# Four-layer sparse graph network on one core: the order of a block's two halves, and feed-forward rows in two buffers

## The chip, the cores and the metric

The kernel runs on one core of one Trainium2 chip. The metric is the device time of one execution in microseconds, given as the median of several runs. The core has a matrix engine (TensorE, in the profile PE, with its weight loads shown apart as PEld), three engines for vectors (VectorE, in the profile DVE; ScalarE, ACT; GpSimd, POOL), and queues that start transfers (SP's queue and GpSimd's). Each engine works through its own list of instructions, and semaphores tie the lists together.

## What is computed

The input is 16 graphs' states on 1024 shared nodes with 128 features, and one 1024 by 1024 adjacency matrix of zeros and ones with about 8 neighbours a node. Four layers follow one another. Layers L0, L2 and L3 are graph transformers with 8 heads of 16, layer L1 is a graph attention layer with one head:

```python
# L0, L2, L3
Q, K, V = h @ Wq, h @ Wk, h @ Wv                 # 8 heads of 16
attn = softmax(where(adj == 0, -inf, Q K^T / sqrt(16)))
x = layer_norm(h + (attn @ V) @ Wo + bo) * ln1_g + ln1_b
y = relu(x @ W1 + b1) @ W2 + b2                  # 128 -> 256 -> 128
x = layer_norm(x + y) * ln2_g + ln2_b
# L1
h = x @ W;  e = leaky_relu(h @ a_src + (h @ a_dst)^T, 0.2)
x = layer_norm(softmax(where(adj == 0, -inf, e)) @ h + x) * ln_gamma + ln_beta
```

## The kernel before

**Tiling.** The kernel works sparsely. A setup turns the adjacency matrix into lists of neighbours, with nodes sorted by degree. After that, a *unit* is one layer, one of two groups of eight graphs, and one of eight tiles of 128 nodes: 4 x 2 x 8 = 64 units in sequence. Within a unit each node's neighbours are handled in *parts* (about six or seven for an attention unit): `gathered` fetches the key and value rows of up to two neighbours a node from a table in DRAM by indirect DMAs (issued by GpSimd, L856), `products` multiplies them by the query on VectorE (L868), `exponentials` sums over each head on VectorE (L891) and takes the exponential on ScalarE (L895), `weighted` multiplies the value rows by it on VectorE (L919), and `summed` adds the rows of a node on TensorE with matrices of marks (L935). When a unit has no more parts, `divided` sums the exponentials on TensorE and divides on VectorE (L972, L975).

**What sets the order.** Everything is written out by hand under a manual schedule; the order of the program is the order of each engine's list. The main loop runs over the parts. Between a part's steps it calls `others()` three times in an attention unit and four times in a graph unit. `others()` opens the *tails* (the rest of the previous unit's layer) at a pace that spreads 15 steps (8 in the graph layer) over the unit, and one further generator (`fronts`: queries of the next unit; `loads`; or `slow`, the second group's entry). A tail is a Python generator, and each `yield` ends a step. `advance(gens)` takes every generator of a list one step further; one such call is an *opening* here.

**Halves and steps.** Each unit has two tails, for its two halves of four graphs: A is h = 0, B is h = 1. B begins with one empty step, so it stands one step behind A. The steps of `attention_tail` are, with the profile's lines:

- 0: transposes of the attention's result (TensorE, L596), copy oT (ScalarE, L598), bias on the layer's input (ScalarE, L640)
- 1: eight matmuls with Wo and the centring matrix into the PSUM tile yps (L644, L645)
- 2: four squares with sums (ScalarE, L580); 3: reciprocal root rstd (GpSimd, L586); 4: four scalings z (ScalarE, L589)
- 5: transposes of z (L596), copy x1 with gain and shift (ScalarE, L600)
- 6: two matmuls with W1 (L655) and two Relus (ScalarE, L659) into the feed-forward rows f1
- 7: eight matmuls with W2 (L664) and four with the centring matrix (L668) into yps
- 8, 9, 10: as 2, 3, 4, for the second norm
- 11: transposes of z, copy xT (L600)
- 12: the store of xT (SP, L530), two matmuls for keys and values and their copy (L538, L542); 13: two more; 14: the store into the next layer's table (SP, L547). In the last layer, 12 transposes back (L596, L598) and 13 writes the output (an indirect DMA of GpSimd, L625).

A matmul in float32 stands in the trace as two records. `graph_tail` has a shorter list: matmuls, squares, rstd, z, then the steps from 11 on with three copies in place of one (L558, L559).

In an opening, the kernel before takes A's step k and then B's step k - 1. So A7 is issued in front of B6, A6 in front of B5, and so on. All feed-forward rows share one buffer: B6's Relus write the rows that A7 has read.

**Other buffers that the change touches.** The pool `smalls` has three buffers for the scores sc, the graph layer's of and the pair both of sums and reciprocals; `exps` has two buffers of exponentials, of 16 x 64 numbers a partition, though a unit needs at most 12 x 64. The larger size is there because the setup's entry (`at_once`, eight blocks, both halves at the same step) borrows these buffers for the second half's keys and values.

Of the kernel before, what the change touches and what calls it, by code (L numbers as in the profile page):

```python
# [12 lines left out]
F32 = mybir.dt.float32  # L13
# [7 lines left out]
P = 128  # L21
D = 128
H = 8
HD = 16
FF = 256
F = FF // P
# [17 lines left out]
G = B // GR  # L44
HF = 2
GH = G // HF
# [4 lines left out]
J = P // 32  # L51
# [37 lines left out]
MOST = max(sum(map(len, _pieces)) for _pieces in PIECES)  # L89
# [33 lines left out]
def sparse_path(ctx: ExitStack, tc: tile.TileContext, a: dict, out: bass.AP, flag):  # L123
# [50 lines left out]
    reps = ctx.enter_context(tc.tile_pool(name="reps", bufs=2))  # L174
    ones_ = ctx.enter_context(tc.tile_pool(name="ones_", bufs=1))
    twos = ctx.enter_context(tc.tile_pool(name="twos", bufs=2))
    exps = ctx.enter_context(tc.tile_pool(name="exps", bufs=2))
    scratch = ctx.enter_context(ExitStack())
    s1 = scratch.enter_context(tc.tile_pool(name="s1", bufs=1))
# [425 lines left out]
    def finish(l, g, t, h, z, gain, shift):  # L605
# [22 lines left out]
            in_=o.rearrange("p g d -> p (g d)"), in_offset=None,  # L628
        )

    def attention_tail(l, g, t, h, o):
        layer = LAYERS[l][0]
        p = {n: w[layer, n] for n in ATTN if (layer, n) in w}
        xt = xs[l, g, t][:, h]
        for _ in range(h):
            yield
        oT = twos.tile([P, GH, P], F32, tag="oT", name="oT")
        turned(o, oT)

        nc.scalar.activation(xt, xt, AF.Identity, bias=p["bo"])  # L640
        yield
        ps = ybanks.tile([P, GH, D], F32, tag="yps", name="yps")
        for i in range(GH):
            nc.tensor.matmul(ps[:, i, :], oT[:, i, :], p["Wo"], start=True, stop=False)  # L644
            nc.tensor.matmul(ps[:, i, :], xt[:, i, :], centre, start=False, stop=True)  # L645
        yield
        z = yield from normed(ps)
        yield
        x1 = twos.tile([P, GH, P], F32, tag="oT", name="x1")
        turned(z, x1, p["ln1_g"], p["ln1_b"])  # L650
        yield
        f1 = ones_.tile([P, F, GH * P], F32, tag="f1", name="f1")
        for f in range(F):
            ps = bank([P, GH * P])
            nc.tensor.matmul(  # L655
                ps, p["W1"][:, f * P : (f + 1) * P], x1.rearrange("p g n -> p (g n)"),
                start=True, stop=True,
            )
            nc.scalar.activation(f1[:, f, :], ps, AF.Relu, bias=p["b1"][:, f : f + 1])  # L659
        yield  # L660
        ps = ybanks.tile([P, GH, D], F32, tag="yps", name="yps")
        for i in range(GH):
            for f in range(F):
                nc.tensor.matmul(  # L664
                    ps[:, i, :], f1[:, f, i * P : (i + 1) * P], p["W2"][:, f, :],
                    start=(f == 0), stop=False,
                )
            nc.tensor.matmul(ps[:, i, :], x1[:, i, :], centre, start=False, stop=True)  # L668
        yield
        z = yield from normed(ps)  # L670
        yield
        yield from finish(l, g, t, h, z, p["ln2_g"], p["ln2_b"])
# [55 lines left out]
    def at_once(g):  # L728

        spare = reps.tile([P, J, ROW], F32, tag="qr", name="spare")  # L730

        def fetch(t):
            if t < T:
                nc.sync.dma_start(
                    spare[:, t % J, :], a["x"][t * P : (t + 1) * P, columns(g, 0, HF)]
                )

        for t in range(3):
            fetch(t)
        yield  # L740
        for t in range(T):
            fetch(t + 3)
            rows = spare[:, t % J, :].rearrange("p (h g d) -> p h g d", h=HF, g=GH)
            both = []
            for h in range(HF):
                kv = None
                if h:
                    kv = exponents()[:, : 2 * GH * D].rearrange("p (c g d) -> p c g d", c=2, g=GH)
                both.append(natural(g, t, h, rows[:, h], kv))
            while both:  # L750
                advance(both)
                yield

    def exponents():
        return exps.tile([P, max(MOST, 2 * D // HD) * G * H], F32, tag="ex", name="ex")


    units = [(l, g, t) for l in range(len(LAYERS)) for g in range(GR) for t in range(T)]
# [40 lines left out]
    def queries(u):  # L799

        l, g, t = units[u]
        if not is_attention(u):
            ps = bank([P, J + 1, G])
            for j in range(J):
                nc.tensor.matmul(ps[:, j, :], rep_of(j, True), srcs[g, t], start=True, stop=True)
            for k, j in enumerate(SHARED[t]):
                at = slice(64 * k, 64 * k + 64)
                nc.tensor.matmul(
                    ps[at, MIX, :], rep_of(j, True)[:, at], srcs[g, t], start=True, stop=True
                )  # L810
            ofs[u] = smalls.tile([P, J + 1, G], F32, tag="of", name="of")
            nc.scalar.copy(ofs[u], ps)
            return
        qs[u] = reps.tile([P, J, ROW], F32, tag="qr", name="qr")
        for h in range(HF):
            q = ones_.tile([P, GH * D], F32, tag="q", name="q")
            ps = bank([P, GH, D])
            for i in range(GH):
                nc.tensor.matmul(
                    ps[:, i, :], xs[l, g, t][:, h, i, :], w[LAYERS[l][0], "Wq"],  # L820
                    start=True, stop=True,
                )
            nc.scalar.copy(q, ps.rearrange("p g d -> p (g d)"))
            yield
            pss = []
            for j in range(J):
                ps = bank([P, GH * D])
                nc.tensor.matmul(ps, rep_of(j), q[32 * j : 32 * j + 32], start=True, stop=True)  # L828
                pss.append(ps)
            for j in range(J):  # L830
                nc.scalar.copy(qs[u][:, j, h * GH * D : (h + 1) * GH * D], pss[j])  # L831
            yield
# [49 lines left out]
    def exponentials(i):  # L882
        u, pieces = parts[i]
        t = units[u][2]
        heads = H if is_attention(u) else 1
        sc = smalls.tile([P, es[i].shape[1], G * heads], F32, tag="sc", name="sc")
        if u not in exs:
            exs[u] = exponents()[:, : MOST * G * heads].rearrange("p (c a) -> p c a", a=G * heads)
        ex, n = exs_of(i)
        if is_attention(u):  # L890
            nc.vector.tensor_reduce(  # L891
                sc[:, :n, :], prs[i][0][:, :n, :].rearrange("p k (a d) -> p k a d", d=HD),
                mybir.AxisListType.X, ALU.add,
            )
            nc.scalar.activation(ex, sc[:, :n, :], AF.Exp, scale=1.0 / HD**0.5)  # L895
        else:
            k = 0
            for piece in pieces:
                m = k + len(piece)
                nc.vector.tensor_tensor(  # L900
                    sc[:, k:m, :], es[i][:, k:m, ROW:], of_piece(ofs[u], piece), ALU.add
                )
                k = m
            nc.vector.scalar_tensor_tensor(
                sc[:, :n, :], sc[:, :n, :], SLOPE, sc[:, :n, :], ALU.mult, ALU.max
            )
            nc.scalar.activation(ex, sc[:, :n, :], AF.Exp)
# [55 lines left out]
    def divided(u):  # L963

        l, g, t = units[u]
        heads, d = (H, HD) if is_attention(u) else (1, D)
        den = bank([P, G * heads])
        for n, c in enumerate(sum(PIECES[t], [])):
            marked(t, c, den, exs[u][:, n, :])
        both = smalls.tile([P, 2, G * heads], F32, tag="both", name="both")  # L970
        yield
        nc.vector.reciprocal(both[:, 1, :], den)  # L972
        for h in range(HF):
            o = twos.tile([P, GH, D], F32, tag="o", name="o")
            nc.vector.tensor_tensor(  # L975
                o.rearrange("p g (a d) -> p (g a) d", d=d),
                accums[u][:, h, :].rearrange("p (a d) -> p a d", d=d),
                both[:, 1, h * GH * heads : (h + 1) * GH * heads]
                .rearrange("p (a o) -> p a o", o=1)
                .to_broadcast([P, GH * heads, d]),  # L980
                ALU.mult,
            )
            tails.append((attention_tail if heads > 1 else graph_tail)(l, g, t, h, o))
        nc.scalar.copy(both[:, 0, :], den)
        n = G * heads
        nc.gpsimd.tensor_tensor(seen[:, :, :n], seen[:, :, :n], both, ALU.add)
# [4 lines left out]
    slow = []  # L991

    def advance(gens):
        for gen in list(gens):
            if next(gen, "end") == "end":
                gens.remove(gen)

# [118 lines left out]
            advance(tails)  # L1116


    fine = smalls.tile([P, 2, G * H], F32, tag="both", name="fine")
    nc.vector.tensor_scalar(fine, seen, LIMIT, None, ALU.is_lt)  # L1120
    counts = const.tile([P, 3], F32, name="counts")
    nc.vector.tensor_reduce(counts[:, 0:1], fine, mybir.AxisListType.XY, ALU.min)
# [428 lines left out]
```

## Time and profile before

| What | Value |
|---|---|
| Median of 3 runs | 2549.46 us (2548.26 to 2554.35) |
| The profiled execution | 2562.74 us |
| Its span in the profile | 2561.0 us |
| Mean granted TensorE clock | 0.911 |
| Time of the first unit's end to the last | from 202 to 2524 us |
| An attention unit, typically | some 40 us |
| A graph unit, on average | some 20 us |
| HBM traffic | 272 GB/s over the span |

The profile is of one execution, 13 us longer than the median. Busy time is counted by engine, and an instruction's idle time is the gap ahead of it on its own engine, with the instruction or transfer that ended it. The chain of work that ended last shows only the last output write of this kernel, so the waits and the timeline have to be read. The profile's slices show no stretch that dominates: after the first tenth (setup) TensorE is busy 7 to 9 tenths in every slice, VectorE 6 to 9, ScalarE 4 to 7, the DMA engines 5 to 9.

### The profile page before, as it was taken

To read this page: it belongs to the slowest core of one execution; us is meant where nothing else is said; L and a number is where in the kernel's file an instruction comes from. 1 tells how busy PE (TensorE), PEld (TensorE's weight loads), DVE (VectorE), ACT (ScalarE), POOL (GpSimd) and SP (SyncE) were. 2 spreads that over 40 slices of the span, in tenths; PEclk is the share of its full clock that TensorE was granted. 3 is DMA by queue.
4 is the path that set the end of the run, shared out by engine and by line. 5 is a ranking of instruction groups with operands and counts; after the bars stand their busy time and mean duration, and the time that the engine had idled before them with its cause. 6 is when DMAs were issued, how large, how long until landed. Compare 5 with 4: busy or idle time off the path is not lost. (4 is left out here: it accounts for less than half of the span.)

```text
span 2561.0 us, 36646 instructions
## 1 busy us (share of the span) xinstructions
PE 2102.6 (82%) x13124; PEld 1303.1 (51%) x13124; DVE 1930.3 (75%) x1470; ACT 1474.6 (58%) x4640; POOL 1450.8 (57%) x978
## 2 busy tenths in 40 slices
PE   6558989788887888988788888988888787888786
PEld 5425656445554554554455554555555454445454
DVE  7887787587877466667887879788797877787782
ACT  3216776565665444455476656667666665566555
POOL 3334666366666588784545545455555656665652
PEclk8679999899898999999899999999999898989888
DMA  7646888667678589898777877788777667567660
GB/s 251 232 170 230 293 280 287 210 227 252 231 257 260 175 282 327 281 322 297 276 256 248 298 258 261 255 283 277 264 267 254 222 240 260 203 222 257 222 222 24
DMA packets 168461, 636.05 MB, mean 248 GB/s; under 512 B 38328, under 2 KB 41144, under 8 KB 119774
## 3 DMA queue, kind: packets, MB, share of 16 engines
q0 software_dynamic: 92672, 485.09, 54.2%
q1 hardware_dynamic: 75600, 148.55, 17.4%
q8 instruction: 105, 1.72, 0.3%
q14 instruction: 84, 0.69, 0.1%
HBM read 603.11 MB, written 92.34 MB: 272 GB/s over the span
## 5 line engine op out<-in xcount | busy, mean ns | idle before, releaser
L856 POOL DMA_INDIRECT e<-table,idx x600 | 925.7, 1543 | 455.9 <-DVE pr L919 245.6
L919 DVE TENSOR_TENSOR pr<-e,ex 128x2048 f32<-128x2048 f32 (+1 forms) x336 | 689.5, 2060 | 205.0 <-ACT ex L895 174.2
L868 DVE TENSOR_TENSOR pr<-e,qr 128x2048 f32<-128x2048 f32 x204 | 460.7, 2258 | 177.8 <-PE acc L935 80.7
L586 POOL TENSOR_TENSOR rstd<-total,power 128x4 f32<-128x4 f32 x224 | 333.1, 1490 | 392.6 <-ACT z L580 385.4
L935 PE MATMUL acc<-pr,marks 128*32 128x512 f32 x2656 | 495.1, 618 | 38.2 <-DVE pr L919 38.2
L891 DVE TENSOR_REDUCE sc<-pr 128x128 f32<-128x2048 f32 (+1 forms) x252 | 518.5, 2058 | 8.6
L580 ACT ACTIVATE z<-yps,root 128x128 f32<-128x128 f32 x896 | 318.5, 378 | 98.5 <-PE yps L683 49.8
L596 PE MATMUL ps<-ident,z 128*128 128x128 f32 x896 | 212.7, 338 | 161.8 <-ACT z L589 161.7
L589 ACT ACTIVATE z<-yps,rstd 128x128 f32<-128x128 f32 x896 | 257.3, 381 | 102.4 <-POOL rstd L586 102.3
L596 PEld LDWEIGHTS ps<-ident,z 128*128 128x128 f32 x896 | 136.0, 159 | 345.4 <-ACT z L589 251.8
L659 ACT ACTIVATE f<-ps,b 128x512 f32<-128x512 f32 x192 | 131.9, 690 | 275.8 <-PE ps L655 275.8
L655 PE MATMUL ps<-x,W 128*128 128x512 f32 x384 | 249.1, 783 | 35.9 <-ACT x L600 35.8
L664 PE MATMUL yps<-W,f 128*128 128x128 f32 x1536 | 259.7, 287 | 17.0 <-ACT f L659 15.9
L664 PEld LDWEIGHTS yps<-W,f 128*128 128x128 f32 x1536 | 212.2, 196 | 77.5 <-ACT f L659 58.6
L935 PEld LDWEIGHTS acc<-pr,marks 128*32 128x32 f32 x2656 | 102.0, 112 | 283.8 <-issue 223.9
L538 PE MATMUL ps<-Wkv,xT 128*128 128x256 f32 x768 | 208.7, 416 | 32.7 <-ACT xT L600 24.1
L831 ACT COPY qr<-ps 128x512 f32<-128x512 f32 x384 | 197.0, 600 | 61.3 <-PE ps L828 55.7
L580 ACT ACTIVATION_READ_ACCUMULATOR z<-yps,root 128x1 f32 x896 | 194.1, 217 | 0.0
L542 ACT COPY kv<-ps 128x512 f32<-128x512 f32 x176 | 103.3, 589 | 140.9 <-PE ps L538 117.1
L538 PEld LDWEIGHTS ps<-Wkv,xT 128*128 128x128 f32 x768 | 146.4, 202 | 73.1 <-ACT xT L600 30.0
L644 PE MATMUL yps<-Wo,oT 128*128 128x128 f32 x768 | 160.9, 292 | 6.0 <-ACT oT L598 6.0
L645 PE MATMUL yps<-centre,x 128*128 128x128 f32 x768 | 158.0, 288 | 6.6
(159 smaller groups left out, 2663.6 us busy)
## 6 DMA issues: line engine op xcount, KB each, us to landing
table<-kv SPq DMA_DIRECT2D x88, 512.0 KB
qx<-qr SPq DMA_DIRECT2D x96, 256.0 KB
kept<-xT SPq DMA_DIRECT2D x96, 256.0 KB
x<-kept SPq DMA_DIRECT2D x48, 512.0 KB
e<-table,idx POOLq DMA_INDIRECT x600
table<-kv SPq DMA_DIRECT2D x32, 256.0 KB
edges<-in_adj SPq DMA_DIRECT2D x8, 512.0 KB
spare<-in_x SPq DMA_DIRECT2D x8, 512.0 KB
```

What stands on the lines that cost most here:

```text
L538: nc.tensor.matmul(ps[:, k, :], x[:, i + k, :], w[LAYERS[l][0], "Wkv"], start=True, stop=True,)
L580: nc.scalar.activation(z[:, i, :], y[:, i, :], AF.Square, scale=D**-0.5, bias=root, accum_out=total[:, i : i + 1],)
L586: nc.gpsimd.tensor_tensor(rstd, total, power, ALU.pow)
L589: nc.scalar.activation(z[:, i, :], y[:, i, :], AF.Copy, scale=rstd[:, i : i + 1])
L596: nc.tensor.transpose(ps[:, i, :], z[:, i, :], ident)
L655: nc.tensor.matmul(ps, p["W1"][:, f * P : (f + 1) * P], x1.rearrange("p g n -> p (g n)"), start=True, stop=True,)
L664: nc.tensor.matmul(ps[:, i, :], f1[:, f, i * P : (i + 1) * P], p["W2"][:, f, :], start=(f == 0), stop=False,)
L856: nc.gpsimd.indirect_dma_start(out=es[i][:, k, :], out_offset=None, in_=tables[l, g][:, :], in_offset=bass.IndirectOffsetOnAxis(ap=idx[:, ...
L868: nc.vector.tensor_tensor(prs[i][0][:, :n, :], es[i][:, :n, :ROW], qx[u].rearrange("p (o c) -> p o c", o=1) if (MIX, 0) in piece else of_p ...
L891: nc.vector.tensor_reduce(sc[:, :n, :], prs[i][0][:, :n, :].rearrange("p k (a d) -> p k a d", d=HD), mybir.AxisListType.X, ALU.add,)
L919: nc.vector.tensor_tensor(prs[i][k0 // 2][:, :m, :].rearrange("p k (a d) -> p k a d", d=d), es[i][:, k0 : k0 + m, base : base + ROW].rearr ...
L935: nc.tensor.matmul(outs[32 * j : 32 * j + 32], marks[:, mark, :], rhss, start=(r == 0 and chunk[0] != MIX), stop=(chunk == last),)
```

## The change

Four edits are made together. In `advance` the generators are taken from the last to the first, so an opening issues B's step k - 1 and then A's step k. The feed-forward rows move from the pool of single buffers to a pool of their own with two. The setup's second half borrows these rows in place of the exponentials' buffers, which shrink to what a unit needs. And sc, of and both move from three buffers to two. The arithmetic is the same.

```diff
+    fs = ctx.enter_context(tc.tile_pool(name="fs", bufs=2))
...
+    def hidden():
+        return fs.tile([P, F, GH * P], F32, tag="f1", name="f1")
...
-        f1 = ones_.tile([P, F, GH * P], F32, tag="f1", name="f1")
+        f1 = hidden()
...
                 if h:
-                    kv = exponents()[:, : 2 * GH * D].rearrange("p (c g d) -> p c g d", c=2, g=GH)
+                    kv = hidden().rearrange("p f (a d) -> p f a d", d=D)
...
     def exponents():
-        return exps.tile([P, max(MOST, 2 * D // HD) * G * H], F32, tag="ex", name="ex")
+        return exps.tile([P, MOST * G * H], F32, tag="ex", name="ex")
...
-            ofs[u] = smalls.tile([P, J + 1, G], F32, tag="of", name="of")
+            ofs[u] = exps.tile([P, J + 1, G], F32, tag="of", name="of")
...
-        sc = smalls.tile([P, es[i].shape[1], G * heads], F32, tag="sc", name="sc")
+        sc = exps.tile([P, es[i].shape[1], G * heads], F32, tag="sc", name="sc")
...
-        both = smalls.tile([P, 2, G * heads], F32, tag="both", name="both")
+        both = exps.tile([P, 2, G * heads], F32, tag="both", name="both")
...
     def advance(gens):
-        for gen in list(gens):
+        for gen in reversed(gens):
             if next(gen, "end") == "end":
                 gens.remove(gen)
...
-    fine = smalls.tile([P, 2, G * H], F32, tag="both", name="fine")
+    fine = exps.tile([P, 2, G * H], F32, tag="both", name="fine")
```

`advance` also serves the setup's entry and the lists of fronts and loads; there at most one generator is left in most openings, or both halves stand at the same step.

## The prediction

> **What bounds the kernel now.** I read the busy shares first, then the list of waits, then the timeline of one attention block of the third layer (L2).
>
> ```profile
> PE 2102.6 (82%) x13124; PEld 1303.1 (51%) x13124; DVE 1930.3 (75%) x1470; ACT 1474.6 (58%) x4640; POOL 1450.8 (57%) x978
> ```
>
> No engine is full; TensorE is nearest. The loss is in waits (us in total, times, longest us):
>
> ```profile
> ACT f L659 <- PE ps L655: 275.8, 176, 5.5
> DVE pr L919 <- ACT ex L895: 174.2, 58, 10.9
> PE ps L596 <- ACT z L589: 161.7, 79, 7.7
> ACT z L589 <- POOL rstd L586: 102.3, 61, 7.6
> DVE pr L868 <- PE acc L935: 92.1, 26, 9.6
> PEld yps L664 <- ACT f L659: 58.6, 95, 0.7
> DVE both L972 <- PE ps L935: 47.8, 24, 9.0
> PEld yps L645 <- ACT x L640: 16.0, 50, 0.3
> ```
>
> The first is ScalarE's Relu waiting for the first feed-forward matmul. Its 192 instances come in 48 groups of four, two per half. Summed by place in the group, the trace's rows give 41.6, 36.4, **189.6** and 8.2 us: step B6's first Relu alone waits 3.95 us a block. The timeline (start us, us) shows why:
>
> ```profile
> 1514.88 0.52 PEld L664 LDWEIGHTS yps<-W,f 128*128 128x128 f32 x4 [0.84 <-issue]
> ...
> 1517.67 1.88 PE L655 MATMUL ps<-x,W 128*128 128x512 f32 x4
> ...
> 1518.73 0.69 ACT L659 ACTIVATE f<-ps,b 128x512 f32<-128x512 f32 x1 [5.05 <-PE ps L655]
> 1519.47 0.30 PEld L664 LDWEIGHTS yps<-W,f 128*128 128x128 f32 x2 [0.75 <-ACT f L659]
> ...
> 1520.17 0.25 ACT L895 ACTIVATE ex<-sc 128x64 f32<-128x64 f32 x1
> ...
> 1520.45 1.23 DVE L919 TENSOR_TENSOR pr<-e,ex 128x1024 f32<-128x1024 f32 x1 [6.13 <-ACT ex L895]
> ```
>
> TensorE runs A7 (L664, L668) from 1514.88 and only then B6's L655. ScalarE stands at B6's Relu meanwhile, the Exp of the next part is queued behind it, and VectorE waits 6.13 us for that Exp. TensorE itself then pauses before B7, whose rows the Relu has just made. By position, 152 of the 174 us that VectorE waits for an Exp end within 4 us of B6's Relu. But then VectorE waits **for TensorE**: 80 of the 92 us at L868 lie 4 to 12 us after that Relu, and in the other blocks it is L972 (the sums of a block, from TensorE) that waits, typically 2.6 us, some 12 us after it. So the Relu stall is the visible one, and TensorE's queue from B6 to the end of the block sets the pace behind it.
>
> **What the Trainium skill says.** "PSUM — Partial Sum Buffer", section "Engine vs sequencer instructions": ScalarE, VectorE and GpSimd run their queues strictly in order, and matmuls start and complete in program order. The trace agrees: the Exp at 1520.17 starts only as the second Relu (1519.59, 0.69 us) ends, although it needs neither Relu. So order within a queue is all that is changed here. "TensorE: Matmul & The Clock Gate", section "What's actually happening": after an idle window of about 3.4 us the clock halves, until activity restores it. The trace agrees: the four L655 records of A6 at 1508.23 take 3.78 us, the same four at 1517.67 take 1.88. A6 runs after the wait for the first norm and pays this in most blocks; the change leaves that wait in place.
>
> **The change, part by part.**
>
> *Buffers.* sc, of and both go from three to two, ex shrinks, the feed-forward rows get two. I cost all at nothing: sc is written again two parts later, after a weighted product (L919) that has already waited for the Exp reading it; of and both are used once a block; the setup's borrowed rows alternate between two buffers as before. If that cover were gone, one VectorE instruction of about 2 us per part would wait. The second f1 buffer is what lets B6 write before A7 has read.
>
> *Queues not touched.* Steps that issue DMAs on SP (12, 14), work on GpSimd (3, 9) or write the output (13 in the last layer) never meet the same kind of step in one opening, so SP's and POOL's order stays. In the setup both halves are at the same step, so only the names swap. Cost nothing.
>
> *B6 ahead of A7.* A7 is 2.72 us of TensorE, B6 1.88, B7 3.3 where 2.72 would do: 0.6 us is the pause for the Relu. Subtracting (2 x 2.72 + 1.88) from the time between A7's start and B7's end, block by block, leaves **24 us** over 48 blocks. After the change A7 covers the Relu and TensorE saves this. ScalarE's Relu, and the Exp behind it, come 2.72 us earlier, up to 48 x 2.72 = 131 us off VectorE's waits. I count none of that beyond TensorE's 0.6: VectorE runs into the waits at L868 or L972, which move only as far as TensorE does. What is late next is A8: its squares (L580) now wait for an A7 that ends 1.9 us later, but they ran only after the late Exp at 1520.3; with A7 ending near 1519.5 they still start 0.6 earlier.
>
> *B5 ahead of A6, B4 ahead of A5.* ScalarE does z of the second half (1.13 us) before the copy x1 of the first (0.78), so A6's matmuls start 0.8 us later, while B5's transposes, formerly after them, go into that gap. Typical block, counted from the first z: before, A6 2.5 to 6.2, B5 to 7.05; after, B5 to 2.9, A6 3.35 to 7.05. Nothing gained or lost, unless B's rstd (L586) is late: before, A6 hid that, now A6 stands behind it. The same sum over all rows gives 16.5 us lost, most of it in nine blocks where rstd ends 2.2 to 6.2 us after z starts. In several of these VectorE isn't held by TensorE; I take half, **8 us**.
>
> *B0 ahead of A1.* The L645 matmuls of B1 no longer wait for L640 (16.0 us); where GpSimd's rstd sets z anyway this is worth nothing, so half: **8 us**. The other hole there, about 1 us of ScalarE before the second oT, closes, but ScalarE then meets TensorE's next result 1 us later: nothing.
>
> *B11 ahead of A12.* A12's matmuls no longer wait 0.87 us for xT (L600) alone, as B11's transposes fill it; but ScalarE does B's z first, so xT comes about 0.4 us later than the earlier start gives back. Net 0.2 us lost in 32 blocks: **6 us**.
>
> *Graph layer and end.* Its A5 waits behind xT for 14 us in all; a few us of that and of the last tail's bare chain: **3 us**.
>
> Sum: 24 + 8 + 3 - 8 - 6 = **21 us** saved. The profiled execution took 2562.74 us (span 2561.0), 13.3 above the median of 2549.46; its stalls are the program's, so I take the difference off the median: 2528.5 us. Bounds: A5/A6 between 0 and 16.5 lost, L645 between 0 and 16, A12 between 13 lost (0.4 x 32) and 10 gained: 24 + 0 + 0 - 16.5 - 13 = 6 slower, to 24 + 16 + 10 + 3 = 53 faster. Two-hop effects on the clock could add or take a half-clock window in some blocks: 3.4 us of matmuls at half speed is 1.7 us, in ten blocks 17 either way.
>
> **Rivals.** *VectorE is the bound.* If L868 and L972 wait for data that also moves up, each block gains the part of its Exp wait that A7 made, about 2.2 of the 3.2 us: 48 x 2.2 = 105, to 2444. For: VectorE's 152 us at one spot. Against: in all but four of the 48 blocks VectorE waits again, for TensorE or a DMA, within 14 us. Chance 0.08.
>
> *No change (2549, within 7.6 us).* The 0.6 us is used up before the block ends: in the last layer GpSimd is busy without a hole from the second half's output write to rstd, and z waits for it (the 102.3 us at L589). If that chain is tied to the landing of the first half's output rather than to B7, nothing arrives. Chance 0.20; that the order isn't changed as said is in it.
>
> *Slower: the second half's z in front of the first half's critical copy.* ScalarE does z of B before x1 of A in both norms, and A6 and A12 are what TensorE needs next. Where B's rstd ends more than about 1.4 us after A's z starts, A6 waits for it with TensorE idle. Today ten blocks are clearly beyond that point; POOL's rstd for B stands behind indirect DMAs, and if faster VectorE work lets those be issued between the two rstd, most blocks go beyond it. Price: 0.8 us more at A6 and 0.8 at A12, less 0.6 at B7, in 48 blocks: +48, and half of them: +24, to 2574. Chance 0.25.
>
> **How the numbers follow.** Forecast 2528, chance 0.47. A measurement of this kernel can tell about 0.3% (7.6 us). Faster 0.47 + 0.08 = 0.55, same 0.20, slower 0.25. The range leaves out the VectorE case and the outer part of the slower one: 2490 (53 saved and some clock) to 2568. The faster cases' own range is 2496 to 2541.
>
> **What would show it.** Right: the third Relu's wait falls from 189.6 to under 100 us, L664's 58.6 nearly vanishes, L580's wait for L668 (46 us) grows, VectorE's wait at L919 falls by 100 and L868 and L972 take up most of it. Wrong: the wait of L596 for L589 (161.7) or of L589 for L586 grows by over 40 us (slower rival), or L868 and L972 don't grow (VectorE rival).

## The result and the profile after

The kernel became slower: 2568.93 us (median of 4 runs, 2567.64 to 2571.23) against 2549.27 us before (4 runs, 2548.26 to 2554.35), a ratio of 1.0074 [1.0057, 1.0092]. The same two kernels on another chip, with more runs, gave 1.0037 [1.0022, 1.0053] (run e6 below). The forecast was 2528, in a range of 2490 to 2568.

The profiled execution took 2571.23 us (span 2569.5) at a mean granted TensorE clock of 0.896; of before it was 2562.74 us, 2561.0 and 0.911. The page's busy shares after:

```profile
PE 2128.9 (83%) x13124; PEld 1301.3 (51%) x13124; DVE 1932.5 (75%) x1470; ACT 1468.6 (57%) x4640; POOL 1449.9 (56%) x978
```

TensorE runs the same 13124 instructions and is busy 26 us longer (2102.6 before): more of them ran at half clock. The trace has records of the granted clock, full or half; those of half clock that begin after the first unit's end add up to 431 us, against 357. The list of waits after (us in total, times, longest):

```profile
PE ps L597 <- ACT z L590: 212.2, 129, 7.6
ACT f L663 <- PE ps L659: 159.5, 185, 2.5
...
ACT z L590 <- POOL rstd L587: 140.0, 72, 8.3
DVE pr L872 <- PE acc L939: 123.3, 27, 9.1
ACT z L581 <- PE yps L672: 122.9, 78, 2.2
...
DVE pr L923 <- ACT ex L899: 115.0, 58, 7.9
...
DVE both L976 <- PE ps L939: 54.3, 20, 12.6
DVE both L976 <- PE ps L539: 34.6, 9, 4.8
...
ACT kv L560 <- DMA table<-kv: 30.2, 6, 6.1
```

Lines are one to four higher than before (L596 is now L597, L589 L590, L586 L587, L655 L659, L919 L923, L935 L939). The Relu's wait (L663) falls from 275.8 to 159.5, VectorE's for an Exp from 174.2 to 115.0, and the W2 matmuls no longer wait for a Relu. But the transposes' wait for z, third of those shown of before, is now the largest of them (161.7 before), and z waits for rstd 140.0 instead of 102.3. The last line is new.

The timeline shows how the two belong together. First the end of one L2 block of the kernel **before**, from A's second z on (start us, length us):

```profile
1768.89 1.16 ACT L589 ACTIVATE z<-yps,rstd 128x128 f32<-128x128 f32 x4
1769.15 1.01 POOL L586 TENSOR_TENSOR rstd<-total,power 128x4 f32<-128x4 f32 x1 [1.73 <-ACT z L580]
...
1769.35 2.29 DVE L868 TENSOR_TENSOR pr<-e,qr 128x2048 f32<-128x2048 f32 x1 [3.26 <-PE acc L935]
...
1770.46 0.78 ACT L600 ACTIVATE xT<-ps,ln_b,ln_g 128x512 f32<-128x512 f32 x1 [0.22 <-PE ps L596]
1771.14 1.13 ACT L589 ACTIVATE z<-yps,rstd 128x128 f32<-128x128 f32 x4
...
1771.30 1.13 PE L538 MATMUL ps<-Wkv,xT 128*128 128x256 f32 x4 [0.87 <-ACT xT L600]
...
1776.08 0.55 DVE L972 RECIPROCAL both<-ps 128x64 f32<-128x64 f32 x1
```

B's rstd takes 1.01 us, A's copy xT runs at 1770.46, B's z after it, and the block's sums are divided 7.2 us after A's z began. The same block **after**:

```profile
1781.09 1.15 ACT L590 ACTIVATE z<-yps,rstd 128x128 f32<-128x128 f32 x4
1781.22 2.29 DVE L872 TENSOR_TENSOR pr<-e,qr 128x2048 f32<-128x2048 f32 x1 [4.95 <-PE acc L939]
1781.36 3.03 POOL L587 TENSOR_TENSOR rstd<-total,power 128x4 f32<-128x4 f32 x1 [1.91 <-ACT z L581]
...
1784.42 1.14 ACT L590 ACTIVATE z<-yps,rstd 128x128 f32<-128x128 f32 x4 [1.97 <-POOL rstd L587]
...
1784.84 1.25 PE L597 MATMUL ps<-ident,z 128*128 128x128 f32 x4 [2.21 <-ACT z L590]
1785.43 1.47 ACT L601 ACTIVATE xT<-ps,ln_b,ln_g 128x512 f32<-128x512 f32 x2
...
1786.28 2.08 PE L539 MATMUL ps<-Wkv,xT 128*128 128x256 f32 x4 [0.19 <-ACT xT L601]
...
1790.92 0.56 DVE L976 RECIPROCAL both<-ps 128x64 f32<-128x64 f32 x1 [2.89 <-PE ps L939]
```

Now rstd of B starts 0.14 us after VectorE's multiply, not 0.20 before it, and takes 3.03 us. ScalarE stands at B's z for it. A's copy, ready to run since A's transposes ended, is queued behind that z; A's matmuls are behind B's transposes on TensorE as well. They come 5.2 us after A's z began instead of 2.4, after the pause at half speed (2.08 us for what took 1.13), and the block is divided 9.8 us after A's z instead of 7.2.

Summed over the 96 norms of the attention blocks, ScalarE's wait at **B's** z is 10 us before and 44 after: 8 to 21 in L0, 2 to 19 in L2, 0 to 3 in L3.

### The profile page after: what moved, and what is told of

Same layout as the page of the kernel before. It is cut to its first block, busy times and chain, and to the rows that moved or that the text cites. A ratio compares the mean times of both kernels' runs of the same rounds, so it can differ in the third digit from the quotient of the medians.

```text
span 2569.5 us, 36732 instructions
## 1 busy us (share of the span) xinstructions
PE 2128.9 (83%) x13124; PEld 1301.3 (51%) x13124; DVE 1932.5 (75%) x1470; ACT 1468.6 (57%) x4640; POOL 1449.9 (56%) x978
## 5 line engine op out<-in xcount | busy, mean ns | idle before, releaser
L860 POOL DMA_INDIRECT e<-table,idx x600 | 949.9, 1583 | 441.1 <-DVE pr L923 230.3
L923 DVE TENSOR_TENSOR pr<-e,ex 128x2048 f32<-128x2048 f32 (+1 forms) x336 | 689.1, 2059 | 145.8 <-ACT ex L899 115.0
L872 DVE TENSOR_TENSOR pr<-e,qr 128x2048 f32<-128x2048 f32 x204 | 461.3, 2261 | 199.0 <-PE acc L939 111.1
L939 PE MATMUL acc<-pr,marks 128*32 128x512 f32 x2656 | 509.7, 629 | 40.7 <-DVE pr L923 40.7
L587 POOL TENSOR_TENSOR rstd<-total,power 128x4 f32<-128x4 f32 x224 | 312.3, 1396 | 380.2 <-ACT z L581 372.3
L597 PE MATMUL ps<-ident,z 128*128 128x128 f32 x896 | 242.0, 362 | 214.9 <-ACT z L590 212.2
L581 ACT ACTIVATE z<-yps,root 128x128 f32<-128x128 f32 x896 | 317.9, 375 | 172.1 <-PE yps L672 122.9
L590 ACT ACTIVATE z<-yps,rstd 128x128 f32<-128x128 f32 x896 | 257.4, 384 | 140.4 <-POOL rstd L587 140.0
L597 PEld LDWEIGHTS ps<-ident,z 128*128 128x128 f32 x896 | 132.5, 152 | 393.6 <-ACT z L590 321.8
L939 PEld LDWEIGHTS acc<-pr,marks 128*32 128x32 f32 x2656 | 103.4, 113 | 315.5 <-issue 247.2
L659 PE MATMUL ps<-x,W 128*128 128x512 f32 x384 | 254.3, 807 | 9.6 <-ACT x L601 9.2
L668 PE MATMUL yps<-W,f 128*128 128x128 f32 x1536 | 234.1, 275 | 0.0
L663 ACT ACTIVATE f<-ps,b 128x512 f32<-128x512 f32 x192 | 131.9, 687 | 162.6 <-PE ps L659 159.5
L668 PEld LDWEIGHTS yps<-W,f 128*128 128x128 f32 x1536 | 206.1, 192 | 23.0 <-issue 23.0
L659 PEld LDWEIGHTS ps<-x,W 128*128 128x128 f32 x384 | 92.2, 260 | 128.4 <-issue 104.1
L648 PE MATMUL yps<-Wo,oT 128*128 128x128 f32 x768 | 153.0, 282 | 0.4 <-ACT oT L599 0.2
```

Of the source, the lines that this page charges most:

```text
L581: nc.scalar.activation(z[:, i, :], y[:, i, :], AF.Square, scale=D**-0.5, bias=root, accum_out=total[:, i : i + 1],)
L587: nc.gpsimd.tensor_tensor(rstd, total, power, ALU.pow)
L590: nc.scalar.activation(z[:, i, :], y[:, i, :], AF.Copy, scale=rstd[:, i : i + 1])
L597: nc.tensor.transpose(ps[:, i, :], z[:, i, :], ident)
L659: nc.tensor.matmul(ps, p["W1"][:, f * P : (f + 1) * P], x1.rearrange("p g n -> p (g n)"), start=True, stop=True,)
L668: nc.tensor.matmul(ps[:, i, :], f1[:, f, i * P : (i + 1) * P], p["W2"][:, f, :], start=(f == 0), stop=False,)
```

## The experiments

The letters in the expectations stand for these theories. **Z**: the second half's z stands in front of the first half's copy and matmuls. **S**: A7 behind B6 makes A's squares late. **M**: the new buffers cost. **C**: the clock halves more, because TensorE catches up and then pauses longer. **K**: in L0's first group, z of B delays the flush of the second group's entry, and a store into the table is waited for.

Kernels in which the order differs have this in place of `advance(tails)`; `opened` is reset where a block's tails are made, so k counts a block's openings. All have the change's buffers but for f1.

```diff
+    def advance_tails():
+        k, attn = opened[0], opened[1] is ATTN
+        opened[0] += 1
+        for gen in reversed(tails) if ORDER else list(tails):
+            if next(gen, "end") == "end":
+                tails.remove(gen)
```

Ratios are to the kernel before on the same chip, with a 95% interval in brackets. Five chips were used: one for e1 to e5, one for e6 to e9, one each for the f, the g and the h runs. A comparison across these groups also holds the difference between chips: the change itself came out at 1.0074 above and at 1.0037 in e6.

**e1, the buffers alone.** `ORDER = False`.

> The changed kernel's buffers with the old order (A before B in every opening). Theory Z (the second half's z in front of the first half's copy costs the time): 2549 us, as before. Theory S (A7 behind B6 makes A8's squares late, and what stands behind them): 2549 us. Theory M (the two-deep buffers or the new places cost it): 2565 to 2570 us.

1.0018 [1.0003, 1.0033]. At most a small cost, about 5 us. With constant matmuls (below), the kernel before's own buffers gave 0.9923 and the new ones 0.9876 and 0.9901, each on another chip, so its sign isn't settled.

**e2, B first in opening 7 alone.** `ORDER = attn and k == 7`.

> The new buffers, and B first in one opening of a block alone, the one with B6 and A7. Theory Z: the 0.6 us a block is saved and nothing is lost, 2525 to 2535 us. Theory S: all of the loss is here, 2565 us or more. Theory M: 2540 to 2570 us, above e1 or equal to it.

1.0032 [1.0015, 1.0048]; half clock 424 us. The swap by itself gains nothing, and the trace suggests why: with A6 ahead of B5, nothing covers B5's copy any more once A7 has left, and the W1 matmuls' wait for it grows from 36.3 (e1) to 53.9 us; nine of the 48 B6 run at half clock, none in e1. So this run doesn't price B6 ahead of A7 as the change has it.

**e3, B first everywhere but at the norms.** `ORDER = k not in ((5, 11) if attn else (4,))`.

> The new buffers, and B first in every opening except those where B's z stands beside A's transposes and copy (openings 5 and 11 of an attention block, 4 of a graph block). Theory Z: 2520 to 2540 us. Theory S: 2565 us or more. Theory M: about 2569 us, as the changed kernel.

1.0069 [1.0043, 1.0094], no better than the change. I took this as the end of Z. It wasn't, as the waits of e3 show beside those of the change:

```profile
PE ps L597 <- ACT z L590: 280.9, 162, 8.6
```

ScalarE's wait at B's z is back at 13 us, but in openings 6 and 12 A's matmuls still stand behind B's transposes on TensorE. The wait only changed its engine: ahead of B's transposes alone TensorE waits 131 us here, 57 with the change and 3 in e1.

**e5, B first at the norms alone.** `ORDER = k in ((5, 11) if attn else (4,))`.

> The new buffers, and B first only in the openings where B's z stands beside A's transposes and copy (5 and 11 of an attention block, 4 of a graph block). Theory Z: all of the loss without the gain of B6 ahead of A7, 2575 to 2597 us. Theory S: 2549 us within 8. Theory M: about 2569 us.

1.0443 [1.0411, 1.0474], by far the slowest of the orders, and slower than any theory had it: z of B in front of A's copy, and neither B5 nor B11 to fill the gap.

```profile
PE ps L659 <- ACT x L601: 84.0, 44, 5.4
```

The W1 matmuls wait 84.0 us for x1, against 36.3 in e1 and 9.2 with the change. To swap the norm's own opening and not the next one is far worse than to swap both.

**e6, the change again**, beside the next three.

> The changed kernel itself, beside the next three on one chip: 1.0074 of the kernel before, within the interval of 1.0057 to 1.0092.

1.0037 [1.0022, 1.0053]. Slower again, by less than expected; half clock 424 us.

**e7 and e8, constant matmuls in the pauses**, in the new order and in the old. They go ahead of the first half's transposes, into the same PSUM bank: two before A5's, one before A11's. The transposes overwrite their results.

```diff
-    def turned(z, dst, gain=None, shift=None):
+    def turned(z, dst, gain=None, shift=None, warm=0):
...
+        for _ in range(warm):
+            nc.tensor.matmul(
+                ps.rearrange("p g n -> p (g n)"), ident,
+                rep.rearrange("p j s n -> p (j s n)"), start=True, stop=True,
+            )
...
-        turned(z, x1, p["ln1_g"], p["ln1_b"])
+        turned(z, x1, p["ln1_g"], p["ln1_b"], 2 if h == 0 else 0)
```

> The changed kernel with idle work for TensorE in its pauses: two 128x512 matmuls of constants ahead of A5's transposes and one ahead of A11's, into the bank that the transposes overwrite. Theory C (the new order lets TensorE catch up, it then pauses longer for the norms, its clock halves more often, and the matmuls after that cost what the swap saved): half-clock time falls by 100 us or more below the changed kernel's 431 us in the main part, and the time is at least 0.3% below that of the next kernel, 2535 to 2555 us. Theory K (what costs is a wait for a buffer of keys and values in the first layer): no lower than the changed kernel, 1.007 or more.

> The old order in the new buffers, with the same idle matmuls. Theory C: half-clock time falls from 339 us as well, but with less to win, 0.3% or more above the kernel with the new order and idle matmuls. Theory K: below the changed kernel by 0.5%, as without the idle matmuls, so 1.000 to 1.004.

0.9922 [0.9894, 0.9950] and 0.9876 [0.9845, 0.9907]. Half clock falls from 424 to 232 us and, in the old order, from 353 (e1) to 195. Both orders gain over 1%, which neither theory had, so the clock matters in this kernel. But it isn't what sets the orders apart: the new one stays behind by 0.46%, though the intervals overlap a little.

**e9, the entry flushed first.** `ORDER = not (entry_ and k == 11)`, where `entry_` marks L0's first group.

> The changed kernel, with A first in opening 11 of the first layer's first group, so that the rest of the second group's entry is flushed ahead of B10's z as it was before. Theory K: the waits for the store into the table (30 us in six) fall below 8 us, the first group of the first layer takes 367 to 372 us in place of 384, and the ratio is 1.002 to 1.004. Theory C: 1.0074 within 0.0015.

1.0012 [0.9993, 1.0031] against 1.0037 of e6 on the same chip; the intervals overlap. The store wait falls, but not below 8 us as expected:

```profile
ACT kv L560 <- DMA table<-kv: 15.2, 3, 6.5
```

In e6 the same wait is 23.3 us in five, and there the first group of L0 takes 371.8 us, in e9 372.2; the 384 us of the expectation stood in the profile of the change alone. So K may be a part, up to a quarter of a per cent, but the profiles don't show the gain where K puts it. The edit also puts A's copy in front of B's z again in that opening, so it doesn't test K alone.

**f1, the kernel before with e7's constant matmuls. f2, the change with one ahead of A11's transposes alone. f3, e9's order with three ahead of A5's and two ahead of A11's** (the numbers handed to `turned`).

> The kernel before, its buffers and its order unchanged, with the same constant 128x512 matmuls into the bank of the transposes as in the two runs before (two ahead of A5's transposes, one ahead of A11's; their results are overwritten by the transposes). Clock theory: 0.985 to 0.989 of the kernel before. Buffer theory (the new buffers cost 0.2%): 0.2% below the old order with the new buffers and the same matmuls (0.9876), so about 0.9855; if the buffers cost nothing, 0.9876.

> The changed kernel with one constant matmul ahead of A11's transposes alone, that is in the one pause in which the change brought new half-clock windows (22 us of them before, 48 to 66 after). Clock theory: about 40 us of half-clock go, and with them 20 us of TensorE time, so the ratio falls from 1.004 to 1.007 to about 0.998, and the half-clock time of the program from about 425 to 385 us. Rival (the slow windows are cover for a wait that would be there anyway): the half-clock time falls, the ratio stays above 1.003.

> The changed kernel with both repairs: A first in the twelfth opening of the first group's units of L0, so that the entry's store is not behind B10's z, and three constant matmuls ahead of A5's transposes and two ahead of A11's. If the store wait (0.25%) and the half-clock are all that the new order costs: 0.988 or lower, level with the old order with constant matmuls (0.9876). If something else in the order costs too: 0.990 to 0.993, as with the constant matmuls alone (0.9922).

0.9923 [0.9898, 0.9948], 1.0027 [1.0004, 1.0050] and 0.9957 [0.9943, 0.9971]. f1 came out above what either of its theories had; it was to settle the buffers' price and, with no old order in the new buffers on its chip, couldn't. f2 missed the clock theory's 0.998: half clock fell to 392 us, and the time hardly followed. f3 missed too: with the wait of L560 for the store gone and half clock at 207 us, nearly as low as in f1 (199), its ratio is still 0.34% above f1's on the same chip, with intervals that overlap. But f3 can't say what was left: TensorE is busy 65 us longer, and the extra constant matmuls alone are 83 us (231 against 148). It left a suspicion of something beside store and clock, no more.

**f4, B first in the last layer alone.** `ORDER = of == 3`, the layer of the tails.

> The new buffers, the old order in L0 to L2, B first only in the openings of the last layer's tails, no constant matmuls. If the forecast's 0.6 us a block arrives where no store and no next layer stands behind it: 8 us less than the new buffers alone (1.0018), so 0.9985, the last layer 8 to 10 us shorter. If the gain is lost there too (half-clock windows after the second norm): 1.002 or more, the last layer as long as before.

0.9984 [0.9968, 1.0000], as expected if the forecast's gain arrives there; the last layer takes 608 us, 618 in e1. This is the layer in which B's z hardly waits for rstd. That brought Z back.

**g1 and g2, no wait for B's rstd**, in the new and in the old order (`ORDER` True and False). Each engine has the same number of instructions.

```diff
         nc.gpsimd.tensor_tensor(rstd, total, power, ALU.pow)
+        if h == 0:
+            firsts["rstd"] = rstd
         yield
+        rstd = firsts["rstd"]
```

> The changed kernel, in which the second half's z is scaled with the first half's rstd (its own is still computed on GpSimd, but not used: the second half's own normalisation is left out). So z of B never waits for GpSimd, and A's copy behind it on ScalarE and A's matmuls behind B's transposes on TensorE don't either. If the late rstd of B is what eats the forecast's 0.6 us a block: clearly faster than the old order with the same edit (next run), by about 20 us, so 0.990 to 0.993 of the kernel before. If it is something else (half-clock, stores): 1.002 to 1.006, as the change itself.

> The same edit (second half scaled with the first half's rstd, its own normalisation left out) with the new buffers and the old order, the reference for the run before. In the old order A's matmuls cover B's rstd, so little is gained: 0.998 to 1.002, if the late rstd is a matter of the new order alone. If the new order's loss is elsewhere, both runs gain alike, and the new order stays 0.2 to 0.5% behind this one.

0.9855 [0.9831, 0.9878] and 0.9988 [0.9970, 1.0006]. This decides it: without that wait the new order is 1.33% faster than the old, about 34 us (0.9855 / 0.9988 = 0.9867), more than the 20 expected. The waits of g1 (z is L595 here, its transposes L602):

```profile
PE ps L602 <- ACT z L595: 159.4, 68, 6.7
...
DVE pr L877 <- PE acc L944: 101.1, 27, 7.1
...
ACT z L595 <- POOL rstd L589: 88.2, 36, 7.3
...
DVE pr L928 <- ACT ex L904: 85.5, 44, 5.9
```

What is left at z is A's. Half clock is 350 us, as in e1 (353) and not as in the change (424 to 431): the extra slow windows were made by the wait. Time by layer from the profiles (us, single executions; from the end of a layer's first unit to that of the next layer's, in L3 to the last unit's end):

| | before | e1 | change | e6 | f4 | g2 (old) | g1 (new) |
|---|---|---|---|---|---|---|---|
| L0 | 702 | 703 | 722 | 700 | 702 | 692 | 674 |
| L1 | 355 | 361 | 351 | 348 | 358 | 349 | 349 |
| L2 | 656 | 647 | 655 | 661 | 648 | 650 | 634 |
| L3 | 619 | 618 | 611 | 609 | 608 | 615 | 605 |
| ScalarE waits at B's z | 10 | 10 | 44 | 45 | 15 | 0 | 0 |
| half clock | 357 | 353 | 431 | 424 | 375 | 340 | 350 |

Single executions differ: the change and e6 are the same kernel, with 722 and 700 us in L0. What stands out of that is L3, 608 to 611 us with the new order and 618 to 619 with the old, where B's z hardly waits. In L0 and L2 the order shows no gain with the wait, and one of 18 and 16 us without it (g1 and g2, on one chip). In L1 the old order alone spreads from 349 to 361 us.

**g3 and g4, both remedies together.** f4's order with e7's constant matmuls, and e8 once more.

> The new buffers, B first only for the tails of the last layer, and the constant matmuls (two ahead of A5's transposes, one ahead of A11's). If what the last layer gains by the order (0.34% of the program without constant matmuls) and what the constant matmuls gain are separate: 0.3% below the old order with constant matmuls on the same chip (next run), so 0.985 to 0.989. If both take out the same pauses: level with it.

> The new buffers in the old order with the constant matmuls once more (0.9876 on another chip; the kernel before's own buffers with them gave 0.9923 on a third), as the reference for the run before: 0.987 to 0.993.

0.9858 [0.9839, 0.9877] and 0.9901 [0.9870, 0.9932]. g3 computes everything and is the fastest such kernel here, 2503.6 us against 2542.5 of the kernel before; that it beats g4 by 0.4% is likely, though the intervals overlap a little.

**h1 and h2, rstd on ScalarE** for the second half, and for both halves with e7's constant matmuls.

```diff
-        nc.gpsimd.tensor_tensor(rstd, total, power, ALU.pow)
+        nc.scalar.activation(rstd, total, AF.Ln)
+        nc.scalar.activation(rstd, rstd, AF.Exp, scale=-0.5)
```

> The changed kernel with the second half's rstd worked out on ScalarE itself (a Ln and an Exp of the 128x4 sums, two short instructions) in place of GpSimd's power, so that z of B stands behind nothing but its own squares; the first half's rstd stays on GpSimd. If the wait for B's rstd is what cost the new order its gain: close to the run in which B borrows A's rstd (0.9855), less two instructions of about 0.25 us twice a block on ScalarE, so 0.985 to 0.990. If that run's gain came from what it left out: 1.000 or more. If ScalarE has to switch tables between Ln and Exp: well above 1.

> The changed kernel with both halves' rstd on ScalarE (Ln and Exp) and the constant matmuls ahead of A5's and A11's transposes: every remedy that the runs support, together. If the rstd wait and the half-clock are separate losses, as the runs so far say: 0.970 to 0.980 of the kernel before. If the matmuls fill the same pauses that the faster rstd closes: 0.982 to 0.990.

1.0987 [1.0964, 1.1010] and 1.2159 [1.2137, 1.2181]: far off, for a reason that the groups of ScalarE in h1 show at once.

```profile
L590 ACT ACT_TABLE_LOAD x112 | 143.7, 1283 | 2.0
L591 ACT ACT_TABLE_LOAD x112 | 143.7, 1283 | 2.0
```

Each Ln, and each Exp behind it, comes with a table load of its own: 287.4 us in h1, where 252.6 us were lost. In h2 it is 448 loads. The Trainium skill, in "ScalarE activation tables: per-element evaluation and per-set limits", section "What a function is on this engine", puts two functions of different sets one load of 1283 ns apart; the rows' mean is 1283. These two runs say nothing about Z. So no run here computes all of B's norm without waiting for GpSimd and is faster for it; rstd on VectorE wasn't tried.

## Why the prediction was wrong, step by step

**B6 ahead of A7: the waits moved as forecast.** The third Relu's wait falls from 189.6 to 58.5 us (forecast: under 100), L668's wait for it is gone, the squares' wait for L672 grows from 46 to 122.9. VectorE's Exp wait falls by 59, not 100, and L872 takes up 31 of it. The 24 us of this step weren't measured by themselves: e2, which has the step alone, gains nothing.

**The gains as a whole: borne out.** 24 + 8 + 3 = 35 us were put on the plus side; g1 against g2 measures 34 for the order with no late rstd, some 8 us either way. That the two agree so well is partly luck: the single terms weren't measured, and the 6 us lost at A12, which the prediction put down to the copy's place and not to rstd, belong in this sum too, which makes it 29.

**B5 ahead of A6 and B11 ahead of A12: this failed.** At A6 the prediction saw the danger, "unless B's rstd (L586) is late", summed it to 16.5 us and took half, 8. At A12 it left a late rstd out of its sum altogether (only its slower rival names both norms): the 6 us there, at most 13, come from the copy's place alone. What the wait takes is 39 to 48 us, half clock in its pauses included: the gains of 34, plus the 5 to 14 us (0.2 to 0.6%) that the new order lies above e1, whichever chip it is taken from. The two terms, 14 us together, were about a third of that, and their bounds too low.

Most of it could be read from the trace of before. The question is when B's rstd ends, and when ScalarE would stand at B's z if A's copy were not in front of it. Counted from the end of the instruction ahead of A's copy, B's rstd of the attention blocks comes 30 us too late in all (19 us at the first norms, 11 at the second), of which the old order shows 10 as waits. The rest was covered by A's copy. After the change the waits are 44 us.

And the length of rstd isn't fixed, which the prediction didn't ask about. Of the 224 in the trace of before, 85 start while one of VectorE's two-input multiplies (L868, L919) runs, and 8 more at most 0.02 us ahead of one that follows a reduction. Each of these 93 ends 0.86 to 0.91 us after that multiply does, however early it started, and so takes up to 3.20 us. The other 131, beside an idle VectorE or its reductions (L891) or started further ahead of a multiply, take 1.00 to 1.05. The Trainium skill states the reason in "SBUF — State Buffer", section "SBUF: two separate sides": a VectorE operation with two SBUF inputs and a GpSimd operation that reads SBUF share a port pair, and the one that starts first has it for its whole length while the other is blocked. The trace agrees as far as rstd goes. That the multiply is blocked in turn isn't seen: it takes 2.29 us as well where an rstd started 0.20 us ahead of it, as at 1769.35 above. After the change, of the 43 us that B's z waits (waits over 0.2 us), 30 are behind an rstd of over 1.5 us, and only 12 behind a short one that the indirect DMAs ahead of it on GpSimd made late, which is what the prediction feared.

**The slower rival: its mechanism was the right one,** but for what makes rstd late, and its sign was there: L597's wait for z grew by 50 us, that of z for rstd by 38. It put 2574 on it; measured were 2569 and, on another chip, 0.37% over the kernel before. It shows block by block: of 93 block times of L2 and L3 in three executions with the new order in those layers (the change, e6, e9), the 41 in which B's z waits no longer than before and in e1 (their mean) got 1.1 us shorter on the mean, the 23 with up to 1 us more wait 0.5 us longer, the 29 with over 1 us more 0.9 us longer.

**Effects on the clock, 17 us either way:** too small. 424 to 431 us of half clock instead of 353 to 357 is 34 to 39 us of TensorE's time; g1, with 350, shows that it follows from the late rstd.

**Buffers at nothing:** 0.18% [0.03, 0.33] more in e1, some 5 us; not confirmed elsewhere.

**Queues not touched:** the order on SP and GpSimd is unchanged, as said. But the *time* of an issue on SP moved: `slow`, the second group's entry, runs behind the tails in an opening, its flush stands behind B10's z on ScalarE, and the copy L560 waits up to 6.1 us for the store of the buffer that it writes. The waits are 30 us in the profile of the change and 23 in e6's; what they cost is not shown (e9).

What stays open: the buffers' price, the store's, and what is left of the 0.46% between e7 and e8 once B's wait is taken out there too; that wasn't run.

## What to carry to other kernels

A step that moves ahead of another on an in-order queue brings its own inputs' lateness with it, and everything behind it inherits that. So price it by when its input arrives, in each stage and at its longest, not by its own length. An input that other work covered until now shows little wait in the profile, here 10 us; its lateness against the moment at which the engine would come to it in the new order can be read from the old trace, here 30 of the 44 us that came. Where a reordering moves little, try it in each layer apart; the layer in which it still gains names the cause by what is missing there.

## What the runs showed of the hardware

A 128x4 power on GpSimd takes 1.00 to 1.05 us. Started while a two-input multiply of VectorE runs, in the trace of before, it ends only 0.86 to 0.91 us after the multiply, up to 3.2 us in all. In the block shown it started 0.14 us behind the multiply, not 0.20 ahead of it, and took 2 us more. Constant matmuls in TensorE's pauses, 144 of them (288 records of 0.62 us), raised the mean granted clock from 0.912 to 0.939 (e1, e8) and left the old order 0.8 to 1.2% below the kernel before on three chips (f1, g4, e8), although they add to TensorE's queue. And Ln and Exp, one behind the other, came with 224 table loads of 1.28 us in h1: one for each of them, as if they did not stand side by side.
